# Two groups' decays in an SBUF buffer, one product less on GpSimd, one output tile less

## The chip, the core and the metric

The kernel runs on one core of one Trainium2 chip. The core has five engines with their own instruction queues: PE (TensorE, matmul), DVE (VectorE), ACT (ScalarE), POOL (GpSimd) and SP (SyncE, which here issues DMAs). They work side by side and wait for each other through semaphores. SBUF is the large on-chip memory; PSUM is a smaller one of eight banks, which PE writes and DVE and ACT also use. The metric is the device time in microseconds, the median of three runs.

## The reference

The input is `x` of shape (8, 192, 64, 64), fp32. The first layer (a two-dimensional gated scan with a projection in and out) is not touched by the change. The second layer normalises the tokens and adds two Mamba blocks, one of them on flipped channels. What matters is the recurrence in a block, with 384 inner channels and 16 states per channel:

```python
dt = softplus(dt @ dt_w.T + dt_b)
A = -exp(A_log)
def step(h, inp):
    dt_t, B_t, C_t, x_t = inp
    dA = exp(dt_t[..., None] * A)
    h = dA * h + (dt_t * x_t)[..., None] * B_t[:, None, :]
    y = einsum('bdn,bn->bd', h, C_t)
    return (h, y)
...
y = ys.transpose(1, 0, 2) + D * xc
y = y * silu(z)
return y @ out_w.T
```

## The kernel before

The two layers run one after the other. The second is cut into passes: 8 images x 8 pieces of 512 tokens (`T`) x 2 Mamba blocks = 128 passes. In a pass the 384 channels are three tiles `c` of 128 partitions, and the 16 states are eight groups `g` of two states (`NG`), so a pass has 24 groups, numbered n = 8c + g. One group is a tile of 128 partitions x 2 states x 512 tokens, 1024 fp32 elements per partition.

For each group five things are done (class `Group`):

- `inputs` (L834), POOL: `hs` = dt*x times B, for all tokens but the first.
- `decays` (L840), ACT: `da` = exp(a*dt), one activation of 512 for each of the two states; then a small copy (L843) of the first token's column into `hs`.
- `scan` (L848), DVE: h = da*h + hs along the 1024 elements, in one instruction. It writes over `da`, or, for a group in `FAR`, over `hs`.
- `keep` (L851), ACT: the last column goes to the state for the next piece.
- `weigh` (L855): the product of h and C, into `hs`, on DVE; for the four groups in `FAR` (0, 12, 15, 20) on POOL, a slot later.
- `sum` (L860), PE: two matmuls with the identity add the product to `yp` in PSUM, three slots after the scan (four for a group in `FAR`).

`da` lies in PSUM, in a pool of two buffers of two banks each; with two banks for general use and two for `yp` all eight banks are taken. `hs` lies in SBUF in ten buffers, B and C (`b_sb`, `c_sb`) in SBUF in eight buffers each, filled by DMAs from SP. So a scan reads `da` from PSUM and `hs` from SBUF, and a product on DVE reads h from PSUM and `c_sb` from SBUF; a product on POOL reads both from SBUF.

The order of the work is written out by hand (`tc.manual_schedule()`, L914): every engine executes its instructions in the order in which the program issues them. One turn of the loop at L947 is a slot, one group's turn on DVE. A slot n issues, in this order: the parts listed in `before[n]`; the inputs of group n+3; the scan of n; the products and sums that are due; the gating of a finished tile (`gated`, L786, DVE); the product of n and `keep` of n; the decays of group n+2; the parts listed in `behind[n]`. The lists (L870 to L911) place all else on slots. Those that count here, by slot of the pass in which they run, for the pass that follows:

- `enter` (L683) at 0 and 8, projections on PE and copies on ACT; `convolve` from 1 to 12.
- `stats` (L622, DVE) at 0 and 3, `root` (L631, ACT) and `newton` (L636, POOL) at 6, in every second pass.
- `gate` (L706) at 13, 14 and 16, a copy of `z` on ACT; `silu` (L711) at 16 on ACT, with an activation table loaded before and after; `low_rank` (L717) at 17 on PE with a copy on ACT.
- `step` (L736), six ACT instructions that make dt, at 1, 9 and 17; `refine` (L753, POOL) and `head` (L766, ACT and POOL) four and five slots later.
- `spread` (L727), the DMAs of B and C, from slot 17 on.
- `project` and `add` (L810): the output tile `y` is written by ACT (first block, L816) at slots 7 and 12 of one pass, added to by DVE (L818) in the next, and stored by SP at slot 13 of that. The pool holds two such tiles.

Which of the two PSUM buffers a group's decays get is chosen when the program is built. In the built program they alternate, but for one place: group 16's decays have the same buffer as group 15's, in all passes but the first. A new tile waits until the readers of the old one in its buffer are done.

Of the kernel before, what the change touches and what calls it, by code (L numbers as in the profile page):

```python
# [8 lines left out]
F32 = mybir.dt.float32  # L9
# [6 lines left out]
P = 128  # L16
CM = 192
# [10 lines left out]
T = 512  # L28
NG = 2
GROUPS = NS // NG  # L30
SLOTS = NC * GROUPS
FAR = (0, 12, 15, 20)
ACT_SET = "natural_log_exp_and_others"
JOINED = 2
UNITS = NC * CHUNK
# [504 lines left out]
def kernel(ctx: ExitStack, tc: tile.TileContext, mid, ln, mambas, out):  # L540
# [9 lines left out]
    p2 = ctx.enter_context(tc.tile_pool(name="l1_p2", bufs=2))  # L550
    ps = ctx.enter_context(tc.tile_pool(name="l1_ps", bufs=2, space=PSUM))
    psd = ctx.enter_context(tc.tile_pool(name="l1_psd", bufs=2, space=PSUM))
    dram = ctx.enter_context(tc.tile_pool(name="l1_dram", bufs=4, space=DRAM))
    bcp = ctx.enter_context(tc.tile_pool(name="l1_bc", bufs=GROUPS))
    hsp = ctx.enter_context(tc.tile_pool(name="l1_hs", bufs=10))

    def bank(name, shape=(P, T)):
        return ps.tile(list(shape), F32, tag="bank", name=name)
# [48 lines left out]
    class Tokens:  # L607
# [4 lines left out]
        def __init__(self, b, k):  # L612
            self.b, self.k, self.tag = b, k, f"{b}_{k}"
# [51 lines left out]
    class Pass:  # L665
# [144 lines left out]
        def add(self, half):  # L810
            t = self.tokens
            if self.i == 0 and half == 0:
                t.y = p2.tile([P, t.slices, CM], F32, tag="y", name=f"y_{t.tag}")
            y = t.y[:, 2 * half : 2 * half + 2, :]
            if self.i == 0:
                nc.scalar.copy(y, self.po)  # L816
            else:
                nc.vector.tensor_add(y, y, self.po)  # L818

    class Group:  # L820

        def __init__(self, n):
            self.p, n = passes[n // SLOTS], n % SLOTS
            self.c, self.g = divmod(n, GROUPS)
            self.far = n in FAR
            self.tag = f"{self.p.tag}_{self.g}_{self.c}"
            self.state = self.p.m.state[:, self.c, self.g * NG : (self.g + 1) * NG]

# [3 lines left out]
            nc.gpsimd.tensor_mul(self.hs[:, :, 1:], dtx, self.p.b_sb[self.g][:, :, 1:])  # L834

        def decays(self):
            self.da = psd.tile([P, NG, T], F32, tag="da", name=f"da_{self.tag}")
            for n in range(NG):
                at = self.g * NG + n
                nc.scalar.activation(  # L840
                    self.da[:, n, :], self.p.dt[self.c], AF.Exp, scale=self.p.m.a[:, self.c, at : at + 1]
                )
            nc.scalar.copy(self.hs[:, :, 0], self.p.first[self.c][:, self.g * NG : (self.g + 1) * NG])  # L843
# [19 lines left out]
    passes = [Pass(t, i) for t in tokens for i in range(2)]  # L863
    groups = [Group(n) for n in range(SLOTS * len(passes))]
# [8 lines left out]
    for n, p in enumerate(passes):  # L873
# [23 lines left out]
        if p.i == 1 and n + 1 < len(passes):  # L897
            t = passes[n + 1].tokens
# [14 lines left out]
    first, t = passes[0], tokens[0]  # L913
    with tc.manual_schedule():  # L914
        t.load()
        t.stats(range(t.slices))
        t.root()
        t.newton()
        t.scale()
        for i in range(2):  # L920
            t.turn(i)
        for c in range(NC):
            first.enter(c)
            first.convolve(c, range(4))
            first.gate(c)
        first.silu()
        first.low_rank()
        for g in range(GROUPS):
            first.spread(0, g)
            first.spread(1, g)  # L930
        first.step(0)
        for part in range(4):
            first.refine(0, part)
        for part in range(2):
            first.head(0, part)

        for n, g in enumerate(groups[:3]):
            g.inputs()
            if n < 2:
                g.decays()  # L940

        def earlier(n, by, far):

            g = groups[n - by] if 0 <= n - by < len(groups) else None
            return g if g and g.far == far else None

        for n in range(len(before)):  # L947
            now = groups[n] if n < len(groups) else None
            for part, args in before[n]:
                part(*args)  # L950
            if n + 3 < len(groups):
                groups[n + 3].inputs()
            if now:
                now.scan()
                if now.far:
                    now.keep()
            if g := earlier(n, 1, True):
                g.weigh()
            for by, far in ((3, False), (4, True)):
                if g := earlier(n, by, far):  # L960
                    g.sum()
            if 4 <= n < len(groups) + 4 and groups[n - 4].g == GROUPS - 1:
                groups[n - 4].p.gated(groups[n - 4].c)
            if now and now.g == 0:
                now.p.accumulate(now.c)
            if now and not now.far:
                now.weigh()
                now.keep()
            if n + 2 < len(groups):
                groups[n + 2].decays()  # L970
            for part, args in behind[n]:
                part(*args)

# [42 lines left out]
def build(arrays):  # L1016
    import concourse.bacc as bacc

    nc = bacc.Bacc("TRN2", target_bir_lowering=False, num_devices=1)
    t = {  # L1020
        k: nc.dram_tensor(f"in_{k}_dram", v.shape, mybir.dt.from_np(v.dtype), kind="ExternalInput").ap()
        for k, v in arrays.items()
    }
    B = arrays["x"].shape[0]
    out = nc.dram_tensor("out_0_dram", (B, L, CM), F32, kind="ExternalOutput").ap()
    with tile.TileContext(nc) as tc, tc.tile_pool(name="mid", bufs=1, space=DRAM) as pool:
        mid = [pool.tile([CM * L], F32, tag=f"mid{b}", name=f"mid{b}") for b in range(B)]
        kernel(
            tc,
            *(t[k] for k in ("x", "w_in", "dw", "vecs", "w_xd", "w_gate", "w_m", "w_out")),  # L1030
            [m.rearrange("(c l) -> c l", l=L) for m in mid],
        )
        names = ("in_w", "conv_w", "vecs", "a_log", "x_w", "dt_w", "out_w")
        kernel(
            tc,
            [m.rearrange("(l c) -> l c", c=CM) for m in mid],
            t["ln"],
            [[t[f"{k}{i}"] for k in names] for i in (1, 2)],
            out,
        )  # L1040
    return nc
# [9 lines left out]
```

## Time and profile before

| | |
|---|---|
| median of 3 runs | 17006.93 us (17002.24 to 17012.62) |
| the profiled execution, own time | 16998.62 us |
| its span, first to last instruction | 16996.8 us |
| mean granted TensorE clock | 0.962 |
| the second layer | from about 6000 us to the end |

In the windows of 2000 us within the second layer:

| us | PE busy | DVE busy | ACT busy | POOL busy | DMA share |
|---|---|---|---|---|---|
| 8000 to 10000 | 1858.48 | 1881.71 | 1514.86 | 1917.39 | 0.28 |
| 10000 to 12000 | 1852.17 | 1883.76 | 1509.66 | 1912.96 | 0.27 |
| 12000 to 14000 | 1860.29 | 1881.41 | 1516.20 | 1915.43 | 0.28 |
| 14000 to 16000 | 1859.87 | 1885.09 | 1507.15 | 1913.53 | 0.28 |

How lines of the profile are read: "L848 DVE TENSOR_TENSOR_SCAN da<-da,hs ... x1875 | 4286.6, 2286 | 366.0 <-ACT hs L843 342.1" is a group of equal instructions by line, engine and operation, with what it writes and reads; then the busy time in us and the mean of one in ns; then how long the engine had stood idle just before such instructions, and which instruction ended that. A timeline line has the start in us, the duration in us, the engine, the line and, in brackets, the idle time before it with its releaser. Where several equal instructions follow each other the timeline merges them (x2, x3), and the duration is that of all together.

### The profile page before, as it was taken

The page shows a single profiled execution, that of the slowest core. Times are in us where ns is not written, and L with a number is a line of the kernel's source. Part 1 is how long each engine was busy: PE and PEld are TensorE (multiplying, and loading weights), DVE is VectorE, ACT ScalarE, POOL GpSimd, SP SyncE. Part 2 cuts the span into 40 slices and gives each one's busy share as a digit, 9 for nine tenths or more (in the row PEclk, how much of TensorE's full clock was granted, in tenths as well). Part 3 has the DMA queues.
Part 4 walks back from the last instruction along what each step waited for, and adds up shares of the span by engine and source line. Part 5 has one row for each costly group of instructions (what it writes and reads, how often), then busy time and mean ns, then how long its engine had stood idle before and what let it go on. Part 6 is the DMA issues. An engine that isn't in the chain of part 4 may idle for free.

```text
span 16996.8 us, 151143 instructions
## 1 busy us (share of the span) xinstructions
PE 15880.5 (93%) x42192; PEld 6479.2 (38%) x42192; DVE 15268.1 (90%) x14474; ACT 11938.6 (70%) x25451; POOL 15164.6 (89%) x9955
## 2 busy tenths in 40 slices
PE   9999999999999989999999999999999999999998
PEld 2333333333333334444444444444444444444443
DVE  8888888888887779999999999999999999999999
ACT  5656666666666667777777777777777777777777
POOL 7787978778787779999999999999999999999999
PEclk8999999999999999999999999999999999999999
DMA  1001010010100022222222222222222222222222
GB/s 30 24 7 30 1 30 9 22 30 1 30 1 26 3 95 105 105 105 105 104 106 104 106 104 106 104 106 104 106 104 106 104 106 104 106 104 103 106 102 87
DMA packets 695389, 1247.33 MB, mean 73 GB/s; under 512 B 311768, under 2 KB 378672, under 8 KB 694544
## 3 DMA queue, kind: packets, MB, share of 16 engines
q1 hardware_dynamic: 694144, 1237.37, 19.9%
q8 instruction: 335, 5.49, 0.1%
q14 instruction: 510, 4.18, 0.1%
q10 hardware_dynamic: 400, 0.29, 0.0%
HBM read 1178.77 MB, written 58.72 MB: 73 GB/s over the span
## 4 chain that ended last, share of the span: by engine, by line
DVE 26%; ACT 9%; POOL 9%; issue 8%; DMA 8%; PE 5%; SPq 0%; DVEq 0%; POOLq 0%; ACTq 0%
DVE da L848 18%; DMA c_sb<-bc 7%; POOL hs L834 6%; ACT da L840 3%; DVE hs L855 3%; DVE hs L848 3%; PE yp L860 2%; PE dbl_ps L721 1%; POOL hs L855 1%; DVE z L786 1%; DMA b_sb<-bc 1%; ACT xc L713 1%; ACT L713 1%; POOL e L756 1%; ACT xt L650 1%
## 5 line engine op out<-in xcount | busy, mean ns | idle before, releaser
L834 POOL TENSOR_TENSOR hs<-dtx,b_sb 128x1022 f32<-128x1022 f32 x3072 | 7140.1, 2351 | 62.1 <-DMA b_sb<-bc 29.8
L848 DVE TENSOR_TENSOR_SCAN da<-da,hs 128x1024 f32<-128x1024 f32 x2560 | 5852.5, 2286 | 497.0 <-ACT hs L843 462.8
L860 PE MATMUL yp<-hs,ident 128*128 128x512 f32 x12288 | 5764.5, 603 | 47.9 <-POOL hs L855 25.4
L840 ACT ACTIVATE da<-dt,a 128x512 f32<-128x512 f32 x6144 | 4246.7, 691 | 435.9 <-DVE hs L848 257.5
L860 PEld LDWEIGHTS yp<-hs,ident 128*128 128x128 f32 x12288 | 2316.7, 193 | 3058.9 <-issue 2700.9
L855 DVE TENSOR_TENSOR hs<-da,c_sb 128x1024 f32<-128x1024 f32 x2560 | 3129.3, 1222 | 88.4
L237 PE MATMUL g<-xp,w_gate_sb 16*128 16x512 f32 x8640 | 1816.2, 658 | 60.4 <-ACT dx L310 51.6
L851 ACT COPY state<-da 128x2 f32<-128x2 f32 x2560 | 399.4, 156 | 1981.8 <-DVE hs L855 1972.8
L700 PE MATMUL pc<-xr,conv_diag 128*128 128x512 f32 x3072 | 1572.3, 642 | 170.4 <-ACT dt L746 151.9
L678 PE MATMUL pi<-xT,in_w 96*128 96x512 f32 x3072 | 1447.2, 597 | 79.3 <-ACT y L816 36.5
L263 DVE TENSOR_TENSOR q<-g,h 128x512 f32<-128x512 f32 x2016 | 1351.4, 684 | 115.5 <-PE g L237 70.0
L273 PE MATMUL q<-q,ident 128*128 128x512 f32 x2688 | 1333.5, 619 | 0.0
L283 ACT ACTIVATE rc<-g,eps 128x512 f32<-128x512 f32 x672 | 462.0, 687 | 1116.7 <-DVE g L278 1116.7
L313 POOL TENSOR_TENSOR dx<-dx,xc 128x512 f32<-128x512 f32 x768 | 1079.5, 1406 | 156.6 <-ACT dx L310 133.6
L848 DVE TENSOR_TENSOR_SCAN hs<-da,hs 128x1024 f32<-128x1024 f32 x512 | 1167.5, 2280 | 57.2 <-POOL hs L834 57.2
L855 POOL TENSOR_TENSOR hs<-hs,c_sb 128x1024 f32<-128x1024 f32 x512 | 1204.9, 2353 | 1.2 <-ACT state L851 1.2
L267 POOL TENSOR_TENSOR q<-q,q 128x512 f32<-128x512 f32 x672 | 852.7, 1269 | 196.5 <-DVE q L263 190.9
L237 PEld LDWEIGHTS g<-xp,w_gate_sb 16*128 16x128 f32 x8640 | 495.0, 188 | 1304.9 <-DVE q L263 394.3
L700 PEld LDWEIGHTS pc<-xr,conv_diag 128*128 128x128 f32 x3072 | 584.8, 198 | 1029.0 <-issue 660.8
L257 POOL TENSOR_TENSOR lam<-lam,xc 128x512 f32<-128x512 f32 x672 | 942.0, 1402 | 33.3 <-ACT lam L254 33.3
L278 DVE TENSOR_TENSOR g<-g,ab 128x512 f32<-128x512 f32 x1344 | 933.0, 694 | 22.8
L196 DVE SCALAR_TENSOR_TENSOR xc<-pi,dw_sb,xc 128x504 f32<-128x504 f32 (+3 forms) x1152 | 839.5, 736 | 98.4 <-POOL xc L162 63.8
(140 smaller groups left out, 22975.2 us busy)
## 6 DMA issues: line engine op xcount, KB each, us to landing
b_sb<-bc SPq DMA_DIRECT2D x1024, 512.0 KB, 9.0
c_sb<-bc SPq DMA_DIRECT2D x1024, 512.0 KB, 8.9
xin<-in_x_dram SPq DMA_DIRECT2D x192, 384.0 KB, 3.6
mid<-ot SPq DMA_DIRECT2D x128, 192.0 KB, 2.1
xt<-mid SPq DMA_DIRECT2D x64, 384.0 KB, 10.0
out_dram<-y SPq DMA_DIRECT2D x64, 384.0 KB, 2.6
bc<-dbl SPq DMA_DIRECT2D x128, 64.0 KB, 1.6
b<-bc SPq DMA_DIRECT2D x128, 8.0 KB, 7.3
```

The costliest lines, as they stand in the source:

```text
L237: nc.tensor.matmul(dst, self.wg[r, at, self.d, :], flat(self.xp[r, self.j]), start=True, stop=True)
L257: nc.gpsimd.tensor_mul(self.lam if self.j else self.hc, self.lam, direction(self.xc, self.d, self.j))
L263: nc.vector.tensor_mul(self.q[i], rows(self.g[i]), self.h[:, :, i : i + HW])
L273: nc.tensor.matmul(self.sum, ident, flat(term), start=(i == 0), stop=(i == 1))
L313: nc.gpsimd.tensor_mul(self.dx, self.dx, direction(self.xc, self.d, self.j))
L678: nc.tensor.matmul(pi, self.m.in_w[:, i, c * P : (c + 1) * P], self.tokens.xT[:, i, :], start=(i == 0), stop=(i == 1))
L700: nc.tensor.matmul(pc, self.m.conv_w[:, c, t, :], self.xr[c][:, t : t + T], start=(t == 0), stop=(t == 3))
L834: nc.gpsimd.tensor_mul(self.hs[:, :, 1:], dtx, self.p.b_sb[self.g][:, :, 1:])
L840: nc.scalar.activation(self.da[:, n, :], self.p.dt[self.c], AF.Exp, scale=self.p.m.a[:, self.c, at : at + 1])
L848: nc.vector.tensor_tensor_scan(h, da, hs, 0.0, ALU.mult, ALU.add)
L855: engine.tensor_mul(self.hs, self.h, self.p.c_sb[self.g])
L860: nc.tensor.matmul(self.p.yp[self.c], ident, self.hs[:, n, :], start=False, stop=stop)
```

## The change

Lines of the kernel move by up to five; the scan is L853 after the change, the decays L845, the product L860.

```diff
-FAR = (0, 12, 15, 20)
+FAR = (0, 12, 20)
+AHEAD = (1, 17)
...
     hsp = ctx.enter_context(tc.tile_pool(name="l1_hs", bufs=10))
+    dap = ctx.enter_context(tc.tile_pool(name="l1_da", bufs=1))
...
-                t.y = p2.tile([P, t.slices, CM], F32, tag="y", name=f"y_{t.tag}")
+                t.y = p2.tile([P, t.slices, CM], F32, tag="y", bufs=1, name=f"y_{t.tag}")
...
             self.far = n in FAR
+            self.ahead = n in AHEAD and self.p is not passes[0]
...
         def decays(self):
-            self.da = psd.tile([P, NG, T], F32, tag="da", name=f"da_{self.tag}")
+            pool = dap if self.ahead else psd
+            self.da = pool.tile([P, NG, T], F32, tag="da", name=f"da_{self.tag}")
...
-            if n + 2 < len(groups):
-                groups[n + 2].decays()
+            for g in groups[n + 2 : n + 4]:
+                if g.ahead == (g is not groups[n + 2]):
+                    g.decays()
```

Group 15's product moves from POOL to DVE, and its sum on PE from slot 19 to slot 18. In every pass but the first, the decays of groups 1 and 17 go to a buffer in SBUF, of which there is one, and are issued a slot sooner: in slot 22 of the pass before, and in slot 14, each behind the decays of the group before it. Their scans then read both inputs from SBUF and write over `da` in SBUF, and their products on DVE read both inputs from SBUF. The output tile `y` has one buffer instead of two.

In the built program of the change, the decays in PSUM alternate between the two buffers without exception: group 16's have group 14's buffer, group 18's have group 15's, group 19's have group 16's.

## The prediction

> **What bounds the kernel now.** I read the page's sums first, then the table by stage of the windows, then the idle column of the groups, then the timelines of DVE, ACT and POOL around the idle, and last the waits in the built programs.
>
> ```profile
> PE 15880.5 (93%) x42192; PEld 6479.2 (38%) x42192; DVE 15268.1 (90%) x14474; ACT 11938.6 (70%) x25451; POOL 15164.6 (89%) x9955
> ...
> DVE  8888888888887779999999999999999999999999
> ...
> POOL 7787978778787779999999999999999999999999
> ```
>
> The second layer is the right part, from about 6000 us on. Three engines share the load, so no single busy share tells the bound. The windows of 2000 us give DVE 1881 and POOL 1917 there. What decides is which engine stands still and for whom.
>
> ```profile
> L848 DVE TENSOR_TENSOR_SCAN da<-da,hs 128x1024 f32<-128x1024 f32 x1875 | 4286.6, 2286 | 366.0 <-ACT hs L843 342.1 <-ACT state L851 23.8
> L855 DVE TENSOR_TENSOR hs<-da,c_sb 128x1024 f32<-128x1024 f32 x1875 | 2292.0, 1222 | 64.7
> L786 DVE TENSOR_TENSOR z<-z,yp 128x512 f32<-128x512 f32 x281 | 189.7, 675 | 32.1 <-PE yp L860 32.1
> ```
>
> These rows cover 8000 to 16000 us, 94 passes. DVE waits 366 / 94 = 3.9 us a pass for ACT's decays. The timeline shows it as two waits in every pass, 1.60 us before scan 16 (12269.72) and 2.25 us before scan 18 (12192.72). The rest of a pass is back to back: scan starts lie 3.465 us apart for a group weighed on DVE (12238.50, 12241.97) and 2.20 us for one weighed on POOL (12200.18, 12202.38). So DVE, with ACT ahead of it twice a pass, sets the time. A pass takes 24 slots, 85.3 us by scan starts. POOL's own work is 28 x 2.31 + 3 x 5.40 (refine) + 3 x 0.48 (head) + 0.97 (newton, 1.94 every second pass) = 83.3 us, so it is only 2 us behind.
>
> **Wait before scan 16.** In the program of before, group 16's decays have the PSUM buffer of group 15, so ACT waits for scan 15 to end:
>
> ```profile
> 12265.96 0.16 ACT L851 COPY state<-da 128x2 f32<-128x2 f32 x1 [0.79 <-DVE hs L855]
> 12268.16 1.42 ACT L840 ACTIVATE da<-dt,a 128x512 f32<-128x512 f32 x2 [2.04 <-DVE hs L848]
> ```
>
> In the changed program they have group 14's, free at 12265.93 when product 14 ends.
>
> **Wait before scan 18.** ACT does silu in slot 16: two table loads and two activations, 12271.71 to 12277.16 = 5.45 us, and only then decays 18.
>
> **The change, slots 14 to 18.** From scan 14 (12262.38) to scan 18 the time is 3.47 + 3.87 + 3.47 + 5.79 = 16.60 us now. After: product 15 comes to DVE, so all four slots are of 3.465 and the dense floor is 13.86. ACT after: keep 14 at 12265.96, decays 16 to 12267.6, decays 17 (moved here) to 12269.1, keep 15 after product 15 at 12269.4, z copy to 12270.1, silu to 12275.6, decays 18 to 12277.4, which is 15.02 after scan 14. So without anything new on DVE, scan 18 comes at 15.02 and 1.58 us are gained; the late thing is still silu, by 1.2 us. Behind the earlier decays 17 on ACT stand only keep 15 and the z copy, and keep 15 waits for product 15 anyway.
>
> **Product 15.** DVE pays 1.265 us more (3.465 - 2.20, inside the 13.86); POOL loses 2.31. Its sum on PE stands a slot earlier, ahead of sum 16, so the gating in slot 19 that waits up to 0.8 us (32.1 / 94 = 0.34 a pass) finds it done: -0.34.
>
> **Group 1.** Its decays move from slot 23 to 22. DVE does not wait there now, so nothing is gained. ACT then has two decays between keep 22 (12209.41) and keep 23 (12212.87): 0.2 + 2 x 1.5 = 3.2 of 3.46 us, so nothing is lost.
>
> **One output tile.** The store is issued in slot 13, lands in 2.6 us, and the next write is 18 slots later, over 60 us. Nothing; if the store's queue (SP) were late by 17 slots it would cost ACT a wait, and no row shows that.
>
> **The third buffer: the unknown.** For groups 1 and 17 the scan and the product read both inputs from SBUF; every big DVE operation of the trace of before has one in PSUM. That is four instructions a pass, 2.28 + 1.22 us twice, beside a POOL that is over 95% busy and reads SBUF. What two inputs from SBUF cost is not in the trace. The nearest rows are DVE operations with no PSUM operand that met a POOL operation:
>
> ```profile
> 787.11 2.42 POOL L162 TENSOR_TENSOR xc<-xc,side 128x504 f32<-128x504 f32 x2 [3.42 <-ACT side L159]
> ...
> 790.95 2.50 POOL L162 TENSOR_TENSOR xc<-xc,side 128x504 f32<-128x504 f32 x2 [1.41 <-ACT side L159]
> ```
>
> ```profile
> 788.86 0.70 DVE L473 TENSOR_SCALAR gr<-gr 128x3 f32<-128x3 f32 x1
> ...
> 790.63 1.77 DVE L482 TENSOR_SCALAR wo<-w_out_sb,gr 128x192 f32<-128x192 f32 x3 [0.20 <-DVE gr L479]
> ```
>
> ```profile
> 5927.13 0.23 DVE L473 TENSOR_SCALAR gr<-gr 128x3 f32<-128x3 f32 x1
> ```
>
> The same 128x3 operation takes 0.23 us with POOL idle, and 0.70 when POOL runs; it then ends at 789.56, and POOL's operation at 787.11 + 2.42 = 789.53. It was held to POOL's end. L482's three take 0.78 us alone (1525.07) and 1.77 here. Against it: statistics L628 read and write SBUF, run inside POOL's L834 (12214.95), and take 0.33 us every time; they read one input and write six elements. The added products are elementwise from SBUF to SBUF, nearest to L473 and L482, so I take exclusion, and keep no cost as the other end.
>
> Price of exclusion per group: POOL's operations start every 2.31 us, so the scan meets one in the middle and waits 1.16 us on average (0 to 2.31). While it runs, POOL's next is held and goes first at its end, since the product waits for the scan: 2.31 more. So 3.47 us on DVE, and POOL is held for 2.20 + 1.20 = 3.4.
>
> [...]
>
> **The sum.** With exclusion, per pass: slots 14 to 18 become 13.86 + 3.47 = 17.33 (silu's 15.02 is covered), +0.73; slot 1 +3.47; slot 19 -0.34; together +3.86. There are 127 passes with such groups: +490 us. The profiled execution took 16998.6 us (span 16996.8), so 17489; the median of the runs, 17006.9, lies 8 us above it, within what runs differ by. POOL's work in that case is 83.3 - 2.31 + 6.8 = 87.8, below DVE's 89.2, so DVE still sets it.
>
> **Rivals.**
> 1. No cost from SBUF inputs. Per pass -1.58 - 0.34 = -1.92, x 127 = -244: 16755, faster. For it: L628, and no DVE row of layer two varies with POOL. Against it: L473 and L482. This ends on the other side; it decides if a scan may read SBUF twice while POOL reads.
> 2. Exclusion, but of another phase. If the scan always comes as POOL ends, DVE pays less and POOL bounds: 87.8 - 85.3 = +2.5 a pass, 17316. If it always just misses, 2 x 1.15 more a pass: 17781.
> 3. Only the products are held, since the scan takes 2.28 us for 1024 elements against 1.22 and so reads at half the pace: 1.16 at slot 1, and at slot 17 it fits under silu's 15.02: -1.58 + 1.16 - 0.34 = -0.76, 16902.
> 4. POOL does not let DVE in between two of its operations (their records overlap by 0.04 us). Then DVE waits for POOL's next wait, the refine of slot 5 or 21: 12227.76 - 12215.88 = 11.9 and 12197.57 - 12186.92 = 10.7. Per pass 22.6 - 2.74 - 0.34 = +19.5: 19470. Against it: L482 ended just as POOL's first of two did, with the second to come.
>
> **How the numbers follow.** Exclusion with any phase (forecast and rival 2) 0.54; rival 1 0.27; rival 3 0.07; rival 4 0.07; something else 0.05, spread evenly. The time is the likeliest case's, 17490, its own range 17316 to 17781. The range reaches from rival 1's 16755, less 15 for rounding, to 17790; rival 4 and half of the rest lie outside. Within 0.2% (34 us, about what a measurement of this kernel can tell from no change) only a mixture of 1 and 2 falls: 0.05. Faster is rival 1, most of 3 and a little of the rest: 0.33. Slower: 0.62.
>
> **What would show it.** Right: scan rows with da in SBUF whose mean is above 3.4 us and the product's near 3.5, POOL's L834 mean up (two to four of 24 longer by 1.2 to 2.3), wait before scan 16 gone, before scan 18 gone, POOL busier than now although it has one product less. Wrong: scan and product with da in SBUF at 2.28 and 1.22 us, and a wait of about 1.2 us left before scan 18 (rival 1); scan at 2.28 and product longer (rival 3); a scan of over 10 us (rival 4). If group 16's decays still waited for DVE's scan 15, or the gating of slot 19 still waited for PE, the gains would be smaller than I say, by 1.6 and 0.34 a pass.

## The result, and the profile after

The changed kernel takes 17424.81 us (median of 4 runs, 17420.52 to 17431.54), before 17008.04 (4 runs): 1.0247 times as long, 95% interval 1.0235 to 1.026. The profiled execution took 17420.52 us, its span is 17418.7. It is slower by 417 us; 490 were forecast.

The page's sums and slices:

```profile
PE 16065.3 (92%) x42192; PEld 6479.5 (37%) x42192; DVE 16217.6 (93%) x14602; ACT 11939.9 (69%) x25451; POOL 15627.1 (90%) x9827
...
DVE  8888888888788599999999999999999999999999
...
POOL 7787877879788599999999999999999999999999
```

DVE is busy 949 us more, yet 128 products more on it are 128 x 1.22 = 156 us. POOL has 128 instructions fewer and is busy 463 us more. Both engines are recorded as busy while they are held: in the stretch shown below, POOL's multiplication of 2.35 us stands in the record with 4.32, and DVE's product of 1.22 with 3.19. The groups of the second layer (8000 to 16000 us):

```profile
L838 POOL TENSOR_TENSOR hs<-dtx,b_sb 128x1022 f32<-128x1022 f32 x2165 | 5433.0, 2539 | 21.9 <-DMA b_sb<-bc 0.8
L853 DVE TENSOR_TENSOR_SCAN da<-da,hs 128x1024 f32<-128x1024 f32 x1894 | 4557.1, 2406 | 0.5 <-issue 0.2 <-ACT da L845 0.2
L860 DVE TENSOR_TENSOR hs<-da,c_sb 128x1024 f32<-128x1024 f32 x1894 | 2671.4, 1410 | 71.2 <-PE yp L865 0.5 <-issue 0.4
L860 POOL TENSOR_TENSOR hs<-hs,c_sb 128x1024 f32<-128x1024 f32 x272 | 776.0, 2853 | 0.0
L853 DVE TENSOR_TENSOR_SCAN hs<-da,hs 128x1024 f32<-128x1024 f32 x271 | 617.8, 2280 | 0.0
L788 DVE TENSOR_TENSOR z<-z,yp 128x512 f32<-128x512 f32 x270 | 181.8, 673 | 0.0
```

The idle time before scans fell from 366 us to 0.5: the waits for ACT are gone, as the change intends. In their place the means grew: scan 2286 to 2406 ns, product 1222 to 1410, POOL's inputs 2351 to 2539. Scans that write to `hs`, which have their decays in PSUM, still take 2280. The gating (L788) no longer waits for PE. The rows of before for POOL and for those scans:

```profile
L834 POOL TENSOR_TENSOR hs<-dtx,b_sb 128x1022 f32<-128x1022 f32 x2250 | 5229.7, 2351 | 41.0 <-DMA b_sb<-bc 17.8 <-PE pi L678 3.7 <-POOL dtx L763 0.2
L855 POOL TENSOR_TENSOR hs<-hs,c_sb 128x1024 f32<-128x1024 f32 x375 | 882.5, 2353 | 0.0
L848 DVE TENSOR_TENSOR_SCAN hs<-da,hs 128x1024 f32<-128x1024 f32 x374 | 852.8, 2280 | 0.0
```

On ACT the decays of group 16 follow the state copy at once, where 2.04 us stood before:

```profile
8063.76 0.16 ACT L856 COPY state<-da 128x2 f32<-128x2 f32 x1 [0.78 <-DVE hs L860]
8063.95 1.42 ACT L845 ACTIVATE da<-dt,a 128x512 f32<-128x512 f32 x2
```

One group 1 on the timelines shows where the time sits. DVE:

```profile
8010.60 3.33 DVE L853 TENSOR_TENSOR_SCAN da<-da,hs 128x1024 f32<-128x1024 f32 x1
8013.96 3.19 DVE L860 TENSOR_TENSOR hs<-da,c_sb 128x1024 f32<-128x1024 f32 x1
8017.08 2.29 DVE L853 TENSOR_TENSOR_SCAN da<-da,hs 128x1024 f32<-128x1024 f32 x1
```

POOL in the same stretch:

```profile
8009.44 2.34 POOL L838 TENSOR_TENSOR hs<-dtx,b_sb 128x1022 f32<-128x1022 f32 x1
8011.75 4.32 POOL L860 TENSOR_TENSOR hs<-hs,c_sb 128x1024 f32<-128x1024 f32 x1
8016.04 7.96 POOL L838 TENSOR_TENSOR hs<-dtx,b_sb 128x1022 f32<-128x1022 f32 x3
```

The scan starts at 8010.60, in the middle of POOL's multiplication, which ends at 8011.78; from there to the scan's end at 8013.93 are 2.15 us, nearly a whole scan (2.28). POOL's next one starts at 8011.75 and takes 4.32 us instead of 2.35: it stands until the scan is done. The product, started at 8013.96, then waits for it (8016.07) and ends at 8017.15; and the first of POOL's next three, merged in the line, takes 3.33 us. Four instructions wait for each other in turn, and none of it shows as idle time. It is so in all 127 passes and for both groups: the scan ends 2.14 to 2.15 us after the multiplication that it met, POOL's next takes 4.31 to 4.37 us and ends 2.13 to 2.16 us after the scan, the product ends 1.08 to 1.09 us after that, and the multiplication behind takes 3.31 to 3.36 us.

Over the 90 or so passes of the window, by the scan starts of each slot:

| per pass, us | before | after | forecast |
|---|---|---|---|
| scan of group 1, mean (least to most) | 2.28 | 3.75 (2.90 to 4.35) | 2.28 + 1.16 |
| its product | 1.22 | 3.19 | 1.22 + 2.31 |
| scan of group 17 | 2.29 | 3.35 (2.37 to 4.00) | 2.28 + 1.16 |
| its product | 1.22 | 3.19 | 1.22 + 2.31 |
| scan 1 to scan 2 | 3.45 | 6.90 | 6.92 |
| scan 14 to scan 18 | 16.60 | 16.89 | 17.33 |
| scan 19 to scan 20 | 4.33 | 3.91 | 3.99 |
| the pass | 85.37 | 88.68 | 89.2 |

3.31 us x 127 passes = 420 us, the difference of the spans (421.9).

### The profile page after: what moved, and what is told of

Read it like the earlier page. It is cut to its first block, busy times and chain, and to the rows that moved or that the text cites. A ratio compares the mean times of both kernels' runs of the same rounds, so it can differ in the third digit from the quotient of the medians.

```text
span 17418.7 us, 151539 instructions
## 1 busy us (share of the span) xinstructions
PE 16065.3 (92%) x42192; PEld 6479.5 (37%) x42192; DVE 16217.6 (93%) x14602; ACT 11939.9 (69%) x25451; POOL 15627.1 (90%) x9827
## 5 line engine op out<-in xcount | busy, mean ns | idle before, releaser
L838 POOL TENSOR_TENSOR hs<-dtx,b_sb 128x1022 f32<-128x1022 f32 x3072 | 7703.7, 2538 | 32.7 <-DMA b_sb<-bc 2.4
L853 DVE TENSOR_TENSOR_SCAN da<-da,hs 128x1024 f32<-128x1024 f32 x2688 | 6466.0, 2405 | 3.1 <-ACT hs L848 2.6
L865 PE MATMUL yp<-hs,ident 128*128 128x512 f32 x12288 | 5824.6, 607 | 211.0 <-DVE hs L860 142.4
L845 ACT ACTIVATE da<-dt,a 128x512 f32<-128x512 f32 x6144 | 4233.4, 693 | 157.9
L860 DVE TENSOR_TENSOR hs<-da,c_sb 128x1024 f32<-128x1024 f32 x2688 | 3785.6, 1408 | 101.2 <-issue 0.9
L856 ACT COPY state<-da 128x2 f32<-128x2 f32 x2688 | 435.2, 162 | 2688.5 <-DVE hs L860 2358.7
L702 PE MATMUL pc<-xr,conv_diag 128*128 128x512 f32 x3072 | 1684.6, 676 | 536.6 <-ACT dt L748 497.9
L680 PE MATMUL pi<-xT,in_w 96*128 96x512 f32 x3072 | 1492.9, 612 | 126.8 <-ACT xT L660 82.2
L860 POOL TENSOR_TENSOR hs<-hs,c_sb 128x1024 f32<-128x1024 f32 x384 | 1093.1, 2847 | 5.4 <-ACT state L856 5.4
L320 DVE TENSOR_TENSOR hu<-g,h 128x512 f32<-128x512 f32 x768 | 523.6, 682 | 441.9 <-PE g L238 439.7
```

The costliest lines, as they stand in the source:

```text
L680: nc.tensor.matmul(pi, self.m.in_w[:, i, c * P : (c + 1) * P], self.tokens.xT[:, i, :], start=(i == 0), stop=(i == 1))
L702: nc.tensor.matmul(pc, self.m.conv_w[:, c, t, :], self.xr[c][:, t : t + T], start=(t == 0), stop=(t == 3))
L845: nc.scalar.activation(self.da[:, n, :], self.p.dt[self.c], AF.Exp, scale=self.p.m.a[:, self.c, at : at + 1])
L853: nc.vector.tensor_tensor_scan(h, da, hs, 0.0, ALU.mult, ALU.add)
L860: engine.tensor_mul(self.hs, self.h, self.p.c_sb[self.g])
L865: nc.tensor.matmul(self.p.yp[self.c], ident, self.hs[:, n, :], start=False, stop=stop)
```

## The experiments

Three explanations of the loss were set against each other. Theory A, from the instance above: a DVE instruction with two SBUF inputs and a GpSimd instruction that reads SBUF shut each other out, the later one standing until the earlier ends (8011.78, 8013.93, 8016.07). Theory B: the loss is the product that came to DVE, with ACT's new order. A third: two SBUF inputs are slow on DVE by themselves.

### Without the SBUF buffer: e1_far_only

```diff
-AHEAD = (1, 17)
+AHEAD = ()
```

> The change without the SBUF buffer: three products on GpSimd and one output tile, decays all in PSUM two slots ahead. Theory A (a DVE instruction with two SBUF inputs and a GpSimd instruction that reads SBUF shut each other out): the whole loss is with the buffer. From scan 14 to scan 18: decays 17 can start only after product 15 (12269.4), so silu ends at 12277.1 and decays 18 at 12278.9, 16.5 us after scan 14 (16.60 before), and slot 19 gains 0.41: -0.5 a pass, about 16930 us. Theory B (the loss is the product that came to DVE, and what ACT does in another order): the loss stays, 17300 or more.

16998.18 us (1.0, interval 0.999 to 1.0009): no difference from before. The loss is with the buffer; B falls (ACT's new order, which e1 gives up with the buffer, stays in e4 below, and that run is faster than before). The half microsecond a pass of gain that was expected, 16930 us, did not come:

```profile
L853 DVE TENSOR_TENSOR_SCAN da<-da,hs 128x1024 f32<-128x1024 f32 x1969 | 4499.8, 2285 | 246.7 <-ACT hs L848 243.2 <-ACT dbl L725 3.0 <-ACT da L845 0.2
L788 DVE TENSOR_TENSOR z<-z,yp 128x512 f32<-128x512 f32 x282 | 190.0, 674 | 0.0
L853 DVE TENSOR_TENSOR_SCAN hs<-da,hs 128x1024 f32<-128x1024 f32 x282 | 643.3, 2281 | 35.9 <-ACT state L856 35.8
```

The first row has one wait of 2.62 us a pass, before scan 18 (16.55 us from scan 14, 16.5 expected). The gating row waits for PE no more (32.1 us before, 0.0 now), but scan 20 now waits 0.38 us for ACT (third row), and scan 19 to 20 is 4.33 us as before: behind the wait that went stood another of the same size.

### One group at a time: e2_ahead17, e3_ahead1

```diff
-AHEAD = (1, 17)
+AHEAD = (17,)
```

> The change with group 17 alone in the SBUF buffer. Theory A: slot 1 loses its 3.44 us a pass, and scan 14 to scan 18 stays at some 16.9: -3.4 x 127 from 17425, about 16990 us (16900 to 17100, by where the scan falls in GpSimd's operation). Theory B: no less than 17300.

16907.41 us (0.9947, interval 0.993 to 0.9963): faster than both kernels. Scan 14 to scan 18 is 16.21 us, the scan is held for 0.39 on average and the product for 1.97.

```diff
-AHEAD = (1, 17)
+AHEAD = (1,)
```

> The change with group 1 alone in the SBUF buffer. Theory A: the time of the three products without the buffer, some 16930, plus 3.44 x 127 = 437: about 17370 us; scan 18 waits 2.3 to 2.6 us for silu again. Theory B: as with both, 17425, or as with none.

17311.01 us (1.0183, interval 1.0168 to 1.0198), 59 us less than expected. Each against the kernel before in its own round, group 17 costs -90 us and group 1 +313, together +223, but both at once cost +417. The difference is in the scans: held for 0.67 us (group 1) and 0.39 (group 17) alone, for 1.47 and 1.06 where both are there. That is (1.47 + 1.06 - 0.67 - 0.39) us x 127 = 187 of the 194. How long a scan is held depends on where it falls in POOL's multiplication: in the change it began 0.21 to 2.20 us before that one's end, and took 2.37 to 4.35 us. That one group's delay moves the other's place is the likely reason, and was not tried by itself.

### GpSimd writes, but does not read: e4_pool_no_read

Inputs of groups 3 to 6 and 19 to 22 and the product of group 0 are left out; a constant is written instead.

```diff
+            self.n = n
...
+            if self.p is not passes[0] and self.n in (3, 4, 5, 6, 19, 20, 21, 22):
+                nc.gpsimd.memset(self.hs[:, :, 1:], 0.5)
+                return
...
+            if self.n == 0 and self.p is not passes[0]:
+                nc.gpsimd.memset(self.hs, 0.5)
+                return
```

> The change, but GpSimd fills with a constant where it would multiply: the inputs of groups 3 to 6 and 19 to 22 and the product of group 0 (so these groups' work is left out). Both groups with decays in SBUF keep their scan and product on DVE. Theory A: with no GpSimd operation beside them that reads SBUF the four instructions take 2.28 and 1.22 us; slot 1 loses 3.44 and scan 14 to scan 18 falls to silu's 15.0 us: -5.3 a pass, about 16750 us. Rival (two inputs from SBUF are slow on DVE in themselves): scans of 3.3 to 3.7 us and products of 3.2 stay, 17350 or more. If GpSimd's writing shuts DVE out as well as its reading: in between, scans held by up to the length of a fill.

16846.22 us (0.991, interval 0.9895 to 0.9924). Group 1 on DVE:

```profile
8083.21 2.27 DVE L857 TENSOR_TENSOR_SCAN da<-da,hs 128x1024 f32<-128x1024 f32 x1
8085.52 1.23 DVE L867 TENSOR_TENSOR hs<-da,c_sb 128x1024 f32<-128x1024 f32 x1
```

and on POOL:

```profile
8082.65 0.95 POOL L864 MEMSET hs<- 128x1024 f32 x1 [0.56 <-ACT state L860]
8083.55 1.84 POOL L839 MEMSET hs<- 128x1022 f32 x2
```

Both inputs from SBUF, full pace. The scan has POOL's fills beside it. POOL stands idle during this product, but in 65 of the 127 passes a fill runs beside group 1's product too, and it never takes over 1.23 us. So two SBUF inputs cost nothing in themselves here (2.27 and 1.23 us), and a GpSimd fill, which only writes, held neither up. The third theory falls. The time is 96 us above the 16750 expected: scan 14 to scan 18 is 15.82 us instead of 15.0, because group 17's product is still 3.19 us long: with the quick fills POOL arrives early at group 23's inputs, which were not replaced. DVE and POOL there:

```profile
8054.64 2.28 DVE L857 TENSOR_TENSOR_SCAN da<-da,hs 128x1024 f32<-128x1024 f32 x1
8056.96 3.19 DVE L867 TENSOR_TENSOR hs<-da,c_sb 128x1024 f32<-128x1024 f32 x1
```

```profile
8051.78 3.62 POOL L839 MEMSET hs<- 128x1022 f32 x4
8055.37 3.70 POOL L842 TENSOR_TENSOR hs<-dtx,b_sb 128x1022 f32<-128x1022 f32 x1
```

The scan goes through beside a fill; the multiplication issued behind it stands until 8056.9 and then holds the product.

### The scan alone, the product alone: e5_scan_only, e11_product_only

```diff
-FAR = (0, 12, 20)
+FAR = (1, 12, 17)
```

> The change with the products of groups 1, 12 and 17 on GpSimd (instead of 0, 12 and 20): of the groups in SBUF only the scan is left on DVE. Theory A: the scans are held by 0 to 2 us as before, and the 1.97 us for which each product was held are gone. Slot 1: 2.2 + 1.5 = 3.7 (3.45 before the change); scan 14 to scan 18: 3 x 3.465 + 2.2 + 0.4 to 1.1 lies under silu's 15.0 (16.60 before); slots 0 and 20 are 1.27 longer each; slot 19 gains 0.4: +0.7 a pass, about 17090 us (17000 to 17150). If the loss came from the scan alone: as long as the change, 17400.

17050.13 us (1.0025, interval 1.0015 to 1.0034). The scans of groups 1 and 17 are 2.99 and 2.77 us on average, the products of the others 1.22. Scan 14 to scan 18 is 14.86 us, silu's bound, which the forecast had at 15.0. So a scan with two SBUF inputs is held, by 0.71 and 0.49 us, also where no product on DVE follows it that reads SBUF twice, and most of the loss goes with the 1.97 us of each product, as Theory A has it.

```diff
-AHEAD = (1, 17)
+AHEAD = ()
...
+            self.into = n == 7
...
-            self.h = self.hs if self.far else self.da
+            self.h = self.hs if self.far or self.into else self.da
...
-                if now.far:
+                if now.far or now.into:
                     now.keep()
...
                 now.weigh()
-                now.keep()
+                if not now.into:
+                    now.keep()
```

> The kernel without an SBUF buffer for decays (three products on GpSimd, 16998 us), with group 7's scan writing over its inputs in SBUF and its product on DVE reading both inputs from SBUF; the scan reads the decays from PSUM. Only this product has two SBUF inputs, and GpSimd is not held by the scan in front of it. Theory A with the order of arrival: it is held for the rest of whatever GpSimd operation it meets, 0 to 2.2 us with a mean near 1, and waits some 0.3 us for the state copy: 1.3 a pass, about 17165 us. If a product with two SBUF inputs is always 1.97 us longer: 2.2 a pass, about 17285. If only the scan's reads clash: 1.22 us as ever, about 17035.

17117.04 us (1.0068, interval 1.0053 to 1.0083). From the answer on the product's line, durations least, median and most in ns:

```profile
L861 DVE TENSOR_TENSOR hs<-da,c_sb x2560: 1207/1224/1226, 6073.0 to 17102.2; 128x1024 f32<-128x1024 f32 x197
L861 DVE TENSOR_TENSOR hs<-hs,c_sb x128: 1224/1261/2942, 6094.9 to 17046.9; 128x1024 f32<-128x1024 f32 x128
```

2560 products with one input in PSUM never exceed 1226 ns; the 128 with both in SBUF take 1224 to 2942 (mean in the window 1911, so 0.69 held). That is less than the mean near 1 that was expected, and the time is 48 us under Theory A's figure. By itself a product is held for 0 to 1.72 us, not for a constant: one that starts at 8078.27 takes 2.68 us, and the three multiplications of POOL from 8075.21 that it meets take 7.93 together, against 6.95 for three in before (12211.60). The 1.97 of the change is the same in every pass, since there the product meets, in all 254 cases, the multiplication that the scan in front had held. The other direction shows in a small POOL operation that meets such a product (8166.81, 1.23 us):

```profile
8165.92 0.23 POOL L641 TENSOR_SCALAR mv<-mv 128x4 f32<-128x4 f32 x1 [2.18 <-ACT rstd L635]
...
8166.81 1.30 POOL L644 TENSOR_SCALAR mv<-mv 128x4 f32<-128x4 f32 x1
```

### Does holding GpSimd back matter? e8_four_far, e10_four_far_alternate

```diff
-FAR = (0, 12, 20)
+FAR = (0, 12, 15, 20)
```

> The change with group 15's product back on GpSimd (four products there). Counted on DVE alone, slot 15 is 1.27 shorter: about 17265 us. Theory A also holds GpSimd back, by 1.98 + 0.99 us for each group in SBUF: its 83.3 us a pass become 89.2, above the 88.7 of the change, so GpSimd sets the time: 17480 or so, no faster than the change, with scans waiting for GpSimd's inputs.

17545.3 us (1.0316, interval 1.0299 to 1.0333), and it tells nothing about POOL: with group 15 on POOL again the built program gave group 16 the buffer of group 15 again, and the wait of 1.60 us before scan 16 was back. So the buffers were tied as well:

```diff
-FAR = (0, 12, 20)
+FAR = (0, 12, 15, 20)
...
-            self.da = pool.tile([P, NG, T], F32, tag="da", name=f"da_{self.tag}")
+            tag = "da" if self.ahead else f"da{(self.n - sum(k < self.n for k in AHEAD) * (self.p is not passes[0])) % 2}"
+            self.da = pool.tile([P, NG, T], F32, tag=tag, bufs=1, name=f"da_{self.tag}")
```

> The change with group 15's product back on GpSimd, and the decays in PSUM tied to alternating buffers, so that group 16 has group 14's again. Counted on DVE alone, scan 14 to scan 18 is 3.46 + 2.20 + 3.46 + 6.5 = 15.6 us (16.89 in the change): 87.4 a pass, 17265 us. If holding GpSimd back matters too (83.3 + 5.9 = 89.2 us of work a pass): 17480 or more, GpSimd nearly without idle time and DVE with waits that end on GpSimd or on ACT behind it.

17477.9 us (1.028, interval 1.0265 to 1.0295). Scan 14 to scan 18 is 15.56 us, as counted, and yet it is no faster than the change. The windows of 8000 to 16000 us, PE, PEld, DVE, ACT and POOL busy; first this kernel:

```profile
8000.00:16000.00 8000.00, 7244.49 (x17777) 3198.80 (x17777) 7746.21 (x4672) 5754.53 (x13221) 7870.51 (x4419) 0.96 0.28 100
```

then the change:

```profile
8000.00:16000.00 8000.00, 7282.32 (x17854) 3183.89 (x17853) 7922.03 (x4783) 5820.06 (x13285) 7705.44 (x4347) 0.97 0.27 101
```

POOL is at 98.4% and sets a pass of 89.1 us, against the 89.2 of work counted for it; in the change DVE stands at 99.0% and POOL at 96.3%. POOL has no wait at all in this window, while DVE idles 185.6 us before its scans; the profile names ACT there, and ACT in turn had stood 4.68 us for POOL's `dtx` in the stretch before one of the scans 23. What the mutual holding adds to POOL has used up its room for a fourth product.

### One output tile: e7_one_tile

```diff
-                t.y = p2.tile([P, t.slices, CM], F32, tag="y", name=f"y_{t.tag}")
+                t.y = p2.tile([P, t.slices, CM], F32, tag="y", bufs=1, name=f"y_{t.tag}")
```

> The kernel before with one output tile instead of two, nothing else. Both theories: the store lands 2.6 us after slot 13 and the next write is 18 slots later: no difference (16980 to 17015).

17000.48 us (1.0001, interval 0.9991 to 1.001). Nothing, as forecast.

### The same waits without SBUF: e6_alternate, e9_alternate_z

```diff
-            self.da = psd.tile([P, NG, T], F32, tag="da", name=f"da_{self.tag}")
+            self.da = psd.tile([P, NG, T], F32, tag=f"da{self.g % 2}", bufs=1, name=f"da_{self.tag}")
```

> The kernel before, with the two PSUM buffers of the decays tied to even and odd groups, so that group 16 has group 14's and not group 15's; nothing else. If the wait before scan 16 is a matter of this buffer: it goes, silu starts 1.6 us sooner, scan 14 to scan 18 is 15.1 us instead of 16.60, a wait of about 2.5 us stays before scan 18: -1.5 a pass, about 16815 us, and GpSimd with 83.3 us of work a pass stands just under DVE's 83.9. If scan 18's decays come at the same time whatever group 16's do: no difference, 16998.

16798.07 us (0.9878, interval 0.9863 to 0.9893). One line in the kernel before, no third buffer:

```profile
L848 DVE TENSOR_TENSOR_SCAN da<-da,hs 128x1024 f32<-128x1024 f32 x1911 | 4366.9, 2285 | 267.2 <-ACT hs L843 136.9 <-POOL hs L834 106.3 <-ACT state L851 24.0
```

The wait before scan 16 is gone, and 2.53 us stay before scan 18; this row also names POOL as releaser. Scan 14 to scan 18 is 15.19 us (15.1 expected).

On top of that edit:

```diff
-        for c, slot in enumerate((13, 14, 16)):
+        for c, slot in enumerate((13, 14, 15)):
```

> The kernel before with the two PSUM buffers tied to even and odd groups, and the last z copy (0.58 us on ACT, with its matmuls) issued in slot 15 instead of 16, where ACT waits for DVE. If silu is what scan 18 waits for: silu starts 0.58 us sooner, the wait of 2.5 us before scan 18 shrinks to 1.95: 83.8 - 0.58 = 83.2 a pass, which is GpSimd's own work (83.3), so about 16745 us, or up to 16770 where GpSimd sets the time. If scan 18 waits for something else than silu: 16798, as with the tied buffers alone.

With the z copy moved as well, 16778.41 us (0.987, interval 0.9853 to 0.9886), the best here and 8 us above the upper end of what was expected. The wait before scan 18 shrank by 0.35 us, not 0.58, and scan 7 waits 0.48 us instead of 0.28. POOL:

```profile
8000.00:16000.00 8000.00, 7463.88 (x18935) 3318.65 (x18934) 7670.81 (x4974) 6180.29 (x14076) 7817.61 (x4700) 0.99 0.28 106
```

It is busy for 97.7% of a pass of 83.67 us, with 83.3 of work counted in its cadence, so it leaves little to win by earlier decays. That POOL took the missing 0.23 us is likely and was not tried by itself.

## Why the prediction was right, point by point

The 417 us lie 73 below the 490, in the direction and by the mechanism that were forecast.

- **Wait before scan 16.** Gone, by the buffer that the built program gave: e6 gains 1.2% by that alone, and e8 loses it again.
- **Wait before scan 18.** Covered by the delay of group 17, as computed. Silu's bound of 15.02 us was 14.86 where DVE came early enough to meet it (e5).
- **Product 15 on DVE.** Scan 15 to 16 went from 3.88 us, wait included, to 3.46.
- **The gating in slot 19.** 0.42 us came off against 0.34, but not for the stated reason, so the size is luck. e1 has product 15's sum a slot earlier, which takes the gating's wait for PE away, and gains nothing there, since ACT is late next. e6 and e10 leave this sum in slot 19, and there scan 19 to 20 is 3.91 to 3.92 us too, without a wait. What goes with the wait is a lateness of PE behind silu, which ACT meets as well at `pd`, where dt is made: 40 times in the window in before, and 40 times in e1 (first and second pair of lines, from the lists of waits), against 0.5 us in all in the change and none in e6. Why PE is in time there was not tried by itself.

```profile
DVE z L786 <- PE yp L860: 32.1, 40, 0.8
ACT e L745 <- PE pd L740: 31.0, 40, 1.0
...
DVE hs L853 <- ACT state L856: 35.8, 40, 0.9
ACT e L747 <- PE pd L742: 30.8, 40, 0.8
```

- **Group 1's earlier decays, one output tile.** Nothing, as said (e7; scan 1 had no wait to lose).
- **Exclusion.** The mechanism held: the scan waits for what it meets (it ends 2.15 us after it), POOL's next is held (4.31 to 4.37 us), goes first at the scan's end and holds the product (3.18 to 3.20 us). That POOL is held in its turn, and then goes first, no row of before shows: it was the author's estimate. The scan's hold of 1.16 us was 1.47 and 1.06; that the two lie on both sides of it is partly luck, since alone they were 0.67 and 0.39 (e3, e2). The mis-sized term is the product's: 2.31 was put in, a full turn of POOL, and 1.97 measured. The multiplication in front ends 2.14 us after the scan, and the product 1.08 after that (8016.07 to 8017.15), 0.14 less than its 1.22. Twice -0.34 for the products, +0.31 and -0.10 for the scans and -0.08 in slot 19 are -0.55, the step from the forecast's 3.86 us a pass to 3.31.
- **The choice between the rows.** The held 128x3 operation (L473) pointed the right way, and the statistics (L628), which read one input, did not count against it. The likeness was thinner than the text says: L473 and L482 multiply one tile by a column of factors, and no run shows why they are held. The small DVE operations of before with two SBUF inputs could not have told: L474 to L479 include four on 128x3 tiles (0.15 to 0.16 us), but POOL is idle beside each of them. What part the two inputs and GpSimd's reading have is shown by the experiments: the product with both inputs in SBUF takes 1.22 to 1.23 us beside fills (e4) and up to 2.94 beside multiplications (e11), and with one in PSUM 1.21 to 1.23 (e11).
- **POOL.** Its hold was put at 3.4 us a group; 4.32 - 2.35 and 3.33 - 2.35 make 2.95. Over the window four of its multiplications a pass are longer, by 1.0 or 2.0 us, 5.98 us in all. It stayed below DVE, as said.

## What to carry to other kernels

Where DVE and GpSimd both run without gaps, count how many inputs of each DVE instruction lie in SBUF before a buffer is moved there from PSUM: beside GpSimd multiplications that read SBUF, a second one made both engines wait in turn here (a scan of 2.28 us took 3.75 and 3.35 on average, a product of 1.22 took 3.19, multiplications of 2.35 took 4.34 and 3.33), and the profile books it as longer instructions, not as idle time (0.5 us before the scans), so compare means by shape. Before a buffer is added for a wait, see in the built program which buffer the waiting tile was given: tying two buffers to even and odd groups took the wait before scan 16 away without a new buffer, and the time with it (16798 us). The prices of two such places need not add: here -90 and +313 us became +417.

## What the runs showed of the hardware that was not expected

- A DVE product with two SBUF inputs holds even a 128x4 GpSimd operation: 1.30 us instead of some 0.22 in the instance shown (e11).
- A GpSimd fill of 128x1024 takes 0.95 us and did not lengthen such DVE instructions (e4); a multiplication of that size takes 2.35 us, and beside it they took up to 4.35 us instead of 2.28 (scan) and 3.20 instead of 1.22 (product) in the change.
- At the change-over the engine that had waited went first: a product issued 0.03 us after its scan still found the multiplication ahead of it, in all 127 passes of the change and for both groups (3.18 to 3.20 us). And no scan was held for more than 2.07 us in the change (4.35 us long) or 2.24 in e5 (4.52), less than one multiplication of 2.35, though POOL had the next one ready behind it.
